# Layer 1's decay matrix: from summed terms and exponentials to spread factors and two scans

## The chip, the core and the metric

The kernel runs on one core of a Trainium2 chip, as one program. The metric is device time in microseconds (us); less is better. The engines are named as in the profile: PE (TensorE matmuls), PEld (its weight loads), DVE (VectorE), ACT (ScalarE), POOL (GpSimd), SP (SyncE, which here only issues DMA).

## The reference

The input is two images of 64 x 64 tokens with 256 channels. Two layers run one after the other, each adding its result to the normalized stream. The change is in layer 1 alone: two passes over the rows and the columns in turn (four calls of `_mamba2` in all), bidirectional, with 8 heads of 64 channels and a state of 64.

```python
def _ssd(xh, dt, A, Bm, Cm):
    cum = jnp.cumsum(dt * A, axis=1)
    diff = cum[:, :, None, :] - cum[:, None, :, :]
    decay = jnp.where(mask, jnp.exp(diff), 0.0)          # mask: lower triangle
    scores = jnp.einsum('bln,bsn->bls', Cm, Bm)[..., None] * decay * dt[:, None, :, :]
    return jnp.einsum('blsh,bshp->blhp', scores, xh)

def _mamba2(x, Win, Wconv, bconv, dt_bias, A_log, D, gn_w, Wout):
    zxbcdt = x @ Win
    z = zxbcdt[..., :DIN]
    xBC = silu(_causal_conv(zxbcdt[..., DIN:DIN + CONVDIM], Wconv, bconv))   # 4 taps
    ...
    dt = softplus(zxbcdt[..., -NHEADS:] + dt_bias)
    A = -jnp.exp(A_log)
    y = _ssd(xh, dt, A, Bm, Cm) + rev(_ssd(rev(xh), rev(dt), A, rev(Bm), rev(Cm)))
    y = y + D[None, None, :, None] * xh
    y = _rmsnorm(y.reshape(b, l, DIN) * silu(z), gn_w)
    return y @ Wout
```

For a sequence of 64 tokens and one head, the decay between two tokens is the product of the factors exp(dt * A) of the tokens between them, in both directions.

## The kernel before

All is fp32. Layer 0 comes first and is not touched by the change. Layer 1 works in 128 blocks: 4 calls (calls 0 and 2 read columns of the image, with a stride, calls 1 and 3 read rows) of 2 images of 16 blocks. A block is 4 sequences of 64 tokens, 256 tokens; two sequences make a pair (q = 0, 1), one on each half of the 128 partitions. In call 3 each block also loads a kept tensor (`y_load`), adds it in `residual` and stores the result.

A block is a list of steps. Each step issues a few instructions, all on one engine:

- PE: `norm_mean`, `x_proj` 0 and 1, `z_proj` 0 and 1, `bc_proj`, `dt_proj` (projections by `Win`), `scores`, `x_transpose` 0 and 1, `decay_sums` 0 and 1, `outputs` (64 small matmuls), `out_proj`, `out_mean`.
- ACT: `norm_squares`; `norm_factor` and `out_factor` (a Ln, then an Exp); `conv_start` and `bc_conv_start` (the last tap of the convolution); `dt_log` (Abs, Exp, Ln: three small instructions); `x_silu`, `z_silu`, `bc_silu` (Silu); `x_copy`; `decays` (Exp in place in PSUM); `out_squares`.
- DVE: `norm_scale`, `conv_taps` 0 and 1 and `bc_conv_taps` (the other three taps, 15 instructions in all, one line in the profile, L1114), `dt_bias`, `dt_sum` (one instruction for dt, then four small ones for `dta`, L1227), `scores_twice`, `mix`, `gated`, `out_scale`.
- POOL: `norm_total`, `decay_terms` (four multiplies of 128 x 512, L1259), `weights` 0 and 1 (a multiply, L1312, and an add, L1318, each), `out_total` (L1375, L1377), `residual` (L1417, in call 3 also L1419).

The decay matrix is made in three steps: `decay_terms` puts dt * A into a triangular mask (`within`), `decay_sums` sums it with matmuls against a second mask (`between`), and `decays` takes the exponential in PSUM. `mix` multiplies it by `weights`.

The order is written by hand in `STEPS`: each step has a time in hundredths of a block's period. Block i's step is issued at 100 i + that time, all blocks' steps sorted together, and every instruction is kept in that order on its engine (`pin`). So in the steady state the queue of an engine holds its steps sorted by time modulo 100, those with a larger time belonging to earlier blocks.

```python
todo = plan([Block(i) for i in range(8 * NBLK)], 100, STEPS)
todo += plan(weights, 2 * NBLK * 100, WEIGHTS, -8)
todo += plan([norm], 0, NORM, -4)
issue(todo)
```

`NORM` holds the group norm of the second image, which runs beside the first blocks: 16 statistics on DVE, 16 `apply` steps on ACT. `WEIGHTS` loads and scales the weights of a call. PSUM has 8 banks, which `bank()` hands out; a tile is given back after its last reader. ACT needs the table of a function loaded (ACT_TABLE_LOAD) before it; most loads are put in where the function that follows isn't in the table at hand, and a load of a common table for Ln and Exp is written out by hand at the end of `bc_silu` (L1251):

```python
pin(nc.scalar.preload_act_table_set(LOG_EXP))
```

Of the kernel before, what the change touches and what calls it, by code (L numbers as in the profile page):

```python
# [13 lines left out]
P = 128  # L14
C = 256
KT = C // P
L = 64
# [207 lines left out]
    (30, "norm_total"),  # L225
    (106, "norm_mean"),
    (129, "norm_factor"),
    (142, "norm_scale"),
    (148, "x_proj", 0),
    (149, "dt_proj"),  # L230
    (157, "conv_start", 0),
    (176, "x_proj", 1),
    (178, "conv_start", 1),
    (179, "dt_bias"),
    (188, "bc_proj"),
    (201, "conv_taps", 0),
    (201, "bc_conv_start"),
    (205, "dt_log"),
    (217, "z_proj", 1),
    (221, "z_proj", 0),  # L240
    (223, "conv_taps", 1),
    (230, "bc_conv_taps"),
    (243, "x_silu"),
    (246, "z_silu"),
    (248, "bc_silu"),
    (251, "x_transpose", 0),
    (252, "scores"),
    (256, "dt_sum"),
    (260, "x_transpose", 1),
    (265, "x_copy", 0),  # L250
    (271, "x_copy", 1),
    (274, "decay_terms"),
    (282, "scores_twice"),
    (287, "weights", 1),
    (289, "decay_sums", 1),
    (302, "decays", 1),
    (305, "decay_sums", 0),
    (313, "weights", 0),
    (315, "decays", 0),
    (324, "mix", 1),  # L260
    (329, "mix", 0),
    (332, "outputs"),
    (356, "gated"),
    (413, "out_squares"),
    (424, "out_total"),
    (428, "out_proj"),
    (448, "out_mean"),
    (454, "out_factor"),
    (460, "out_scale"),
    (480, "y_load"),  # L270
    (559, "residual"),
# [86 lines left out]
class Consts:  # L358
    def __init__(self, nc, pool):
        def tile_(shape, name):  # L360
            return pool.tile(shape, F32, name=name, tag=name)
# [40 lines left out]

        self.between = tile_([P, L], "between")
        self.within = tile_([P, L], "within")
        for t, op, mult in ((self.between, ALU.is_gt, 1), (self.within, ALU.is_ge, -1)):
            nc.gpsimd.memset(t, 1.0)
            for half, sign in ((0, mult), (1, -mult)):
                rows = t[half * L : (half + 1) * L, :]  # L410
                nc.gpsimd.affine_select(
                    out=rows,
                    in_=rows,
                    compare_op=op,
                    fill=0.0,
                    base=0,
                    pattern=[[-sign, L]],
                    channel_multiplier=sign,
                )
# [592 lines left out]
def layer1(tc, k, d, U, kept, out):  # L1012
# [7 lines left out]
    with ExitStack() as ctx:  # L1020
# [5 lines left out]
        ps = ctx.enter_context(tc.tile_pool(name="l1_ps", bufs=8, space=PSUM))  # L1026
        pin = tc.keep_in_program_order

# [6 lines left out]
        class Weights:  # L1035
# [5 lines left out]
            def load(self):  # L1041
# [14 lines left out]
                self.heads = wp.tile([P, 2, NH], F32, name="heads")  # L1056
                nc.sync.dma_start(out=self.heads, in_=d[self.ax + "_heads"][self.li : self.li + 1].to_broadcast([P, 2, NH]))
# [26 lines left out]
            def decay_rates(self):  # L1084
                self.neg_a = wp.tile([P, NH], F32, name="neg_a")
                act(self.neg_a, self.heads[:, 1, :], AF.Exp)
                pin(nc.vector.tensor_scalar(self.neg_a, self.neg_a, -1.0, None, ALU.mult))
# [22 lines left out]
        def taps(dst, pp, w):  # L1110
            dsts, pps = seqs(dst), seqs(pp)
            for j in range(1, TAPS):
                pin(
                    nc.vector.scalar_tensor_tensor(  # L1114
                        dsts[:, :, j:],
                        pps[:, :, : L - j],
                        w[:, TAPS - 1 - j : TAPS - j],
                        dsts[:, :, j:],
                        ALU.mult,
                        ALU.add,  # L1120
                    )
                )
# [4 lines left out]
        class Block:  # L1127
# [48 lines left out]
            def conv_taps(self, h):  # L1176
                for j in range(2):
                    c = 2 * h + j
                    taps(self.conv[:, c, :], half_of(self.px[h], j), self.w.cols[:, c, :])
# [8 lines left out]

            def bc_conv_taps(self):
                taps(self.conv_bc, self.pbc, self.w.bc_cols)  # L1190
# [16 lines left out]
            def dt_bias(self):  # L1207
                self.dt = two.tile([P, NPAIR, NH], F32, name="dt")
                bias = self.w.heads[:, 0:1, :].to_broadcast([P, NPAIR, NH])
                pin(nc.vector.tensor_add(self.dt, self.pdt, bias))  # L1210
# [7 lines left out]
            def dt_sum(self):  # L1218
                dt = self.dt
                pin(nc.vector.scalar_tensor_tensor(dt, dt, 0.0, self.log, ALU.max, ALU.add))  # L1220
                dta = two.tile([P, NPAIR, 2, NH], F32, name="dta")
                for e in range(2):
                    rows = slice(e * L, (e + 1) * L)
                    a = self.w.neg_a[rows].unsqueeze(1).to_broadcast([L, NPAIR, NH])
                    for half in range(2):
                        to = slice(half * L, (half + 1) * L)
                        pin(nc.vector.tensor_mul(dta[to, :, e, :], dt[rows], a))  # L1227
                self.dta = dta.rearrange("p q e h -> p (q e) h")
# [23 lines left out]


            def decay_terms(self):
                self.terms = []
                for s in range(SB):
                    terms = two.tile([P, NH, L], F32, name=f"terms{s}", tag=f"terms{s}")
                    pin(
                        nc.gpsimd.tensor_mul(  # L1259
                            terms,  # L1260
                            self.dta[:, s, :].unsqueeze(2).to_broadcast([P, NH, L]),
                            k.within.unsqueeze(1).to_broadcast([P, NH, L]),
                        )
                    )
                    self.terms.append(terms)
# [57 lines left out]
            def decay_sums(self, q):  # L1323
                self.seg = getattr(self, "seg", {})
                self.seg[q] = bank()
                for e in range(2):
                    matmul(
                        self.seg[q][e * L : (e + 1) * L],
                        k.between,
                        self.terms[2 * q + e].rearrange("p h l -> p (h l)"),  # L1330
                        True,
                        True,
                    )

            def decays(self, q):
                act(self.seg[q], self.seg[q], AF.Exp)

            def mix(self, q):
                self.mixes = getattr(self, "mixes", {})
                self.mixes[q] = two.tile([P, NH, L], F32, name=f"mix{q}", tag=f"mix{q}")  # L1340
                seg = self.seg[q].rearrange("p (h l) -> p h l", l=L)
                pin(nc.vector.tensor_mul(self.mixes[q], seg, self.weight[q]))
# [167 lines left out]
```

## Time and profile before

| | |
|---|---|
| median of 3 runs | 8551.74 us (8551.55 to 8555.54) |
| span of the profiled execution | 8553.2 us (no other time is given for it) |
| PE busy | 8258.4 us, 97% |
| DVE busy | 7426.7 us, 87% |
| ACT busy | 6797.4 us, 79% |
| POOL busy | 7588.4 us, 89% |
| chain that ended last, by line | PE L1033 25% of the span, PE L1273 2%, the rest under 1% each |

The profile is of one execution. Busy shares are means over both layers, so they are read by stage, in windows of the span. A group of instructions has a line of `kernel.py`, an engine, the operation and its tiles (output <- inputs); lines L1030 and L1033 are the helpers `act` and `matmul`, so there the tiles tell the step. fp32 matmuls have two records each, and their ends are modelled: on PE the time from one start to the next is read.

### The profile page before, as it was taken

The numbers are of one execution on the slowest core, as the hardware profiler recorded it, in microseconds if no ns is written. First come the engines' busy times: TensorE is split into PE (matmuls) and PEld (weight loads), VectorE is DVE, ScalarE is ACT, GpSimd is POOL, SyncE is SP. The second block draws the span as 40 slices with busy tenths as digits, with TensorE's granted clock in tenths as the row PEclk, the third lists the DMA queues.
The fourth block names the chain that finished last, engine by engine and source line by source line (L and its number), as shares of the span: only waits on it lengthen the run. The fifth ranks groups of instructions, "written<-read, shape, count | busy, mean of one in ns | idle before, by whom it ended". The sixth has DMA issues, their size and how long they took to land. (4 is left out here: it accounts for less than half of the span.)

```text
span 8553.2 us, 159162 instructions
## 1 busy us (share of the span) xinstructions
PE 8258.4 (97%) x60752; PEld 7001.5 (82%) x60752; DVE 7426.7 (87%) x7179; ACT 6797.4 (79%) x11826; POOL 7588.4 (89%) x4426
## 2 busy tenths in 40 slices
PE   8999999999999999999999999999889999999999
PEld 6888888888888888888888888888777777777777
DVE  6999999999999999999998999999977777777776
ACT  5888888888888778888887888888768777777776
POOL 6999999999999999999999999999957777777777
PEclk9999999999999999999999999999999999999999
DMA  4443444444444444444444444444410000000001
GB/s 137 137 137 128 135 137 136 137 132 134 138 129 133 149 140 155 130 134 136 136 131 132 139 134 136 130 132 136 145 53 1 7 4 1 10 1 1 16 31 33
DMA packets 495562, 878.17 MB, mean 103 GB/s; under 512 B 69200, under 2 KB 85584, under 8 KB 493264
## 3 DMA queue, kind: packets, MB, share of 16 engines
q1 hardware_dynamic: 479296, 846.29, 31.6%
q10 hardware_dynamic: 15504, 21.71, 0.8%
q8 instruction: 480, 7.86, 0.4%
q14 instruction: 282, 2.31, 0.1%
HBM read 844.71 MB, written 23.07 MB: 101 GB/s over the span
## 5 line engine op out<-in xcount | busy, mean ns | idle before, releaser
L876 POOL TENSOR_TENSOR prod<-prod,c_row 128x1024 f32<-128x1024 f32 x1280 | 3005.3, 2369 | 89.7 <-DVE prod L865 85.4
L846 POOL TENSOR_TENSOR b<-dtx,b_row 128x1024 f32<-128x1024 f32 x1024 | 2417.1, 2374 | 177.5 <-DVE prod L865 160.3
L538 PE MATMUL ps_y<-ident,prod 128*128 128x128 f32 x16384 | 2088.2, 276 | 65.8 <-POOL prod L876 53.2
L538 PEld LDWEIGHTS ps_y<-ident,prod 128*128 128x128 f32 x16384 | 1842.5, 142 | 295.3 <-POOL prod L876 139.8
L531 ACT ACTIVATE ps_h<-dt,neg_a 128x512 f32<-128x512 f32 x2048 | 1408.4, 688 | 471.0 <-DVE prod L879 360.2
L865 DVE TENSOR_TENSOR_SCAN prod<-ps_h,b 128x1024 f32<-128x1024 f32 x768 | 1732.0, 2275 | 55.7 <-POOL b L846 31.8
L531 ACT ACTIVATE b<-dt,neg_a 128x512 f32<-128x512 f32 x2048 | 1356.9, 711 | 79.7 <-DVE prod L865 77.0
L531 ACT ACTIVATE scaled<-dtxt,bt 128x256 f32<-128x256 f32 x2560 | 1089.5, 497 | 305.3 <-PE ps_h L538 294.2
L865 DVE TENSOR_TENSOR_SCAN ps_h<-b,ps_h 128x1024 f32<-128x1024 f32 x512 | 1170.3, 2286 | 143.1 <-PE ps_h L534 91.5
L865 DVE TENSOR_TENSOR_SCAN prod<-b,ps_h 128x1024 f32<-128x1024 f32 x512 | 1167.6, 2281 | 58.6 <-PE ps_h L538 35.2
L1033 PE MATMUL ps_mm<-xn,w_in 128*128 128x256 f32 x4608 | 1063.6, 381 | 12.9 <-DVE xn L1154 12.9
L879 DVE TENSOR_TENSOR prod<-ps_h,c_row 128x1024 f32<-128x1024 f32 x768 | 940.7, 1225 | 154.9 <-DVE ps_h L865 83.8
L1259 POOL TENSOR_TENSOR terms<-dta,within 128x512 f32<-128x512 f32 x512 | 524.0, 1044 | 541.8 <-DVE dta L1227 527.7
L1033 PEld LDWEIGHTS ps_mm<-xn,w_in 128*128 128x128 f32 x4608 | 868.9, 191 | 128.2 <-DVE xn L1154 13.9
L534 PE MATMUL ps_mm<-xi,diag_w 128*128 128x256 f32 (+3 forms) x4096 | 918.2, 374 | 1.5 <-ACT xi L531 1.5
L534 PE MATMUL ps_h<-diag,dtxt 128*128 128x128 f32 x6144 | 764.5, 278 | 90.1 <-DVE prod L879 61.3
L534 PEld LDWEIGHTS ps_h<-diag,dtxt 128*128 128x128 f32 x6144 | 724.7, 193 | 134.6 <-ACT ps_h L531 75.1
L534 PEld LDWEIGHTS ps_mm<-xi,diag_w 128*128 128x128 f32 x4096 | 753.1, 190 | 80.7 <-issue 1.5
L538 PE MATMUL ps_h<-ident,scaled 128*128 128x128 f32 x5120 | 693.3, 280 | 73.7 <-DVE prod L879 51.0
L1114 DVE SCALAR_TENSOR_TENSOR conv<-ps_mm,cols,conv 128x252 f32<-128x252 f32 (+2 forms) x1536 | 705.3, 474 | 63.9 <-ACT conv L1030 27.6
L538 PEld LDWEIGHTS ps_h<-ident,scaled 128*128 128x128 f32 x5120 | 583.0, 144 | 179.7 <-ACT b L531 71.1
L865 DVE TENSOR_TENSOR_SCAN ps_h<-ps_h,b 128x1024 f32<-128x1024 f32 x256 | 583.4, 2279 | 0.2 <-ACT ps_h L531 0.2
(144 smaller groups left out, 12212.5 us busy)
## 6 DMA issues: line engine op xcount, KB each, us to landing
c_row<-bc_rows SPq DMA_DIRECT2D x2048, 256.0 KB, 3.3
b_row<-bc_rows SPq DMA_DIRECT2D x1024, 256.0 KB, 3.3
y_in<-y SPq DMA_DIRECT2D x32, 256.0 KB, 2.9
out_dram<-y_in SPq DMA_DIRECT2D x32, 256.0 KB, 2.5
XU<-in_x_dram SPq DMA_DIRECT2D x8, 512.0 KB, 7.3
bc_rows<-dbc SPq DMA_DIRECT2D x128, 32.0 KB, 2.8
XU<-in_x_dram ACTq DMA_DIRECT2D x8, 512.0 KB, 5.5
y<-Y ACTq DMA_DIRECT2D x8, 512.0 KB, 5.1
```

What stands on the lines that cost most here:

```text
L531: pin(nc.scalar.activation(*args, **kwargs))
L534: pin(nc.tensor.matmul(out, lhsT=lhsT, rhs=rhs, start=start, stop=stop))
L538: nc.tensor.matmul(out, lhsT=x, rhs=order, start=start, stop=stop, is_transpose=True)
L846: pin(nc.gpsimd.tensor_mul(b, self.dtx[u], self.row(u, 0, n)))
L865: nc.vector.tensor_tensor_scan(*(t.rearrange("p c t -> p (c t)") for t in (to, a, b)), 0.0, ALU.mult, ALU.add,)
L876: pin(nc.gpsimd.tensor_mul(prod, prod, self.row(u, 1, n)))
L879: pin(nc.vector.tensor_mul(prod, self.h[u, n], self.row(u, 1, n)))
L1033: pin(nc.tensor.matmul(out, lhsT=lhsT, rhs=rhs, start=start, stop=stop))
L1114: nc.vector.scalar_tensor_tensor(dsts[:, :, j:], pps[:, :, : L - j], w[:, TAPS - 1 - j : TAPS - j], dsts[:, :, j:], ALU.mult, ALU.add,)
L1259: nc.gpsimd.tensor_mul(terms, self.dta[:, s, :].unsqueeze(2).to_broadcast([P, NH, L]), k.within.unsqueeze(1).to_broadcast([P, NH, L]),)
```

## The change

The matrix is now built from the factors. `dt_turn` transposes dt on PE, `factors` takes exp(dt * A) on ACT in one instruction of 16 partitions x 128, writes the rows to DRAM with two DMAs and reads them back with two more, each of which spreads a row of 16 x 65 numbers over 64 partitions (`spread`; the 65th number of each group is zero). `decay_after` runs along `spread` from a unit matrix (`units`) with a scan (multiply, then max), and `decay_before` runs a second one in the other direction over the result of the first. Both are DVE instructions of 128 x 1040. `mix` moves from DVE to POOL. `decay_terms`, `decay_sums`, `decays`, the four `dta` instructions and the masks `within` and `between` go. `taps` now goes through the tiles of a `conv_taps` step in turn, tap by tap, and the taps of `bc_conv_taps` are part of `conv_taps` 1. The loads of bias and rates in `Weights` are split in three. `STEPS` has new times throughout.

The diff, cut (removed masks, context and blank lines are left out):

```diff
@@ -222,53 +222,51 @@
 STEPS = (
     (0, "norm_squares"),
-    (30, "norm_total"),
-    (106, "norm_mean"),
-    (129, "norm_factor"),
-    (142, "norm_scale"),
-    (148, "x_proj", 0),
-    (149, "dt_proj"),
-    (157, "conv_start", 0),
-    (176, "x_proj", 1),
-    (178, "conv_start", 1),
-    (179, "dt_bias"),
-    (188, "bc_proj"),
-    (201, "conv_taps", 0),
-    (201, "bc_conv_start"),
-    (205, "dt_log"),
-    (217, "z_proj", 1),
-    (221, "z_proj", 0),
-    (223, "conv_taps", 1),
-    (230, "bc_conv_taps"),
-    (243, "x_silu"),
-    (246, "z_silu"),
-    (248, "bc_silu"),
-    (251, "x_transpose", 0),
-    (252, "scores"),
-    (256, "dt_sum"),
-    (260, "x_transpose", 1),
-    (265, "x_copy", 0),
-    (271, "x_copy", 1),
-    (274, "decay_terms"),
-    (282, "scores_twice"),
-    (287, "weights", 1),
-    (289, "decay_sums", 1),
-    (302, "decays", 1),
-    (305, "decay_sums", 0),
-    (313, "weights", 0),
-    (315, "decays", 0),
-    (324, "mix", 1),
-    (329, "mix", 0),
-    (332, "outputs"),
-    (356, "gated"),
-    (413, "out_squares"),
-    (424, "out_total"),
-    (428, "out_proj"),
-    (448, "out_mean"),
-    (454, "out_factor"),
-    (460, "out_scale"),
-    (480, "y_load"),
-    (559, "residual"),
+    (58.2, "norm_total"),
+    (58.6, "norm_mean"),
+    (100.9, "norm_factor"),
+    (108.4, "norm_scale"),
+    (112.4, "dt_proj"),
+    (118.4, "bc_proj"),
+    (132, "dt_bias"),
+    (141.2, "bc_conv_start"),
+    (145.8, "x_proj", 0),
+    (146.3, "dt_log"),
+    (149, "x_proj", 1),
+    (149.7, "z_proj", 1),
+    (151.9, "conv_start", 0),
+    (157.4, "conv_start", 1),
+    (167.2, "conv_taps", 0),
+    (172.6, "dt_sum"),
+    (189.8, "dt_turn"),
+    (199.9, "conv_taps", 1),
+    (217.3, "z_proj", 0),
+    (218.3, "factors"),
+    (224.8, "bc_silu"),
+    (271.8, "z_silu"),
+    (300.5, "scores"),
+    (316.3, "scores_twice"),
+    (319.8, "y_load"),
+    (320.1, "x_silu"),
+    (325, "weights", 1),
+    (327.2, "weights", 0),
+    (329.8, "decay_after"),
+    (336.1, "x_transpose", 0),
+    (341, "x_copy", 0),
+    (347.7, "x_transpose", 1),
+    (354.5, "x_copy", 1),
+    (362.7, "decay_before"),
+    (364.8, "mix", 0),
+    (393.3, "mix", 1),
+    (395.1, "outputs"),
+    (417, "gated"),
+    (427.2, "out_squares"),
+    (469.6, "out_proj"),
+    (514.4, "out_total"),
+    (529.4, "out_mean"),
+    (532.9, "out_factor"),
+    (534.3, "out_scale"),
+    (546.6, "residual"),
 )
...
@@ -1024,7 +1004,17 @@
+        dram = ctx.enter_context(tc.tile_pool(name="l1_dram", bufs=3, space=bass.MemoryType.DRAM))
+        units = one.tile([P, NPAIR * NH, L + 1], F32, name="units")
+        nc.vector.memset(units[:, :, L:], 0.0)
+        nc.vector.tensor_copy(
+            units[:, :, :L], k.eye.unsqueeze(1).to_broadcast([P, NPAIR * NH, L])
+        )
+        factors = [one.tile([NPAIR * NH, 2, L + 1], F32, name=f"factors{j}") for j in range(2)]
+        for t in factors:
+            nc.vector.memset(t, 0.0)
@@ -1053,8 +1043,14 @@
-                self.heads = wp.tile([P, 2, NH], F32, name="heads")
-                nc.sync.dma_start(out=self.heads, in_=d[self.ax + "_heads"][self.li : self.li + 1].to_broadcast([P, 2, NH]))
+                heads = d[self.ax + "_heads"][self.li]
+                self.bias = wp.tile([P, NH], F32, name="bias")
+                nc.sync.dma_start(out=self.bias, in_=heads[0:1].to_broadcast([P, NH]))
+                self.neg_a = wp.tile([NPAIR * NH, 1], F32, name="neg_a")
+                for q in range(NPAIR):
+                    nc.sync.dma_start(
+                        out=self.neg_a[q * NH : (q + 1) * NH], in_=heads[1:2].rearrange("o h -> h o")
+                    )
@@ -1082,8 +1078,7 @@
-                self.neg_a = wp.tile([P, NH], F32, name="neg_a")
-                act(self.neg_a, self.heads[:, 1, :], AF.Exp)
+                act(self.neg_a, self.neg_a, AF.Exp)
@@ -1107,19 +1102,20 @@
-        def taps(dst, pp, w):
-            dsts, pps = seqs(dst), seqs(pp)
+        def taps(parts):
-                pin(
-                    nc.vector.scalar_tensor_tensor(
-                        dsts[:, :, j:],
-                        pps[:, :, : L - j],
-                        w[:, TAPS - 1 - j : TAPS - j],
-                        dsts[:, :, j:],
-                        ALU.mult,
-                        ALU.add,
-                    )
-                )
+                for dst, pp, w in parts:
+                    to = seqs(dst)[:, :, j:]
+                    pin(
+                        nc.vector.scalar_tensor_tensor(
+                            to,
+                            seqs(pp)[:, :, : L - j],
+                            w[:, TAPS - 1 - j : TAPS - j],
+                            to,
+                            ALU.mult,
+                            ALU.add,
+                        )
+                    )
         def last_tap(dst, pp, w):
@@ -1174,9 +1170,10 @@
             def conv_taps(self, h):
-                for j in range(2):
-                    c = 2 * h + j
-                    taps(self.conv[:, c, :], half_of(self.px[h], j), self.w.cols[:, c, :])
+                parts = [(self.conv[:, 2 * h + j, :], half_of(self.px[h], j), self.w.cols[:, 2 * h + j, :]) for j in range(2)]
+                if h:
+                    parts.append((self.conv_bc, self.pbc, self.w.bc_cols))
+                taps(parts)
             def bc_proj(self):
@@ -1185,9 +1182,6 @@
             def bc_conv_start(self):
-            def bc_conv_taps(self):
-                taps(self.conv_bc, self.pbc, self.w.bc_cols)
@@ -1206,7 +1200,7 @@
             def dt_bias(self):
-                bias = self.w.heads[:, 0:1, :].to_broadcast([P, NPAIR, NH])
+                bias = self.w.bias.unsqueeze(1).to_broadcast([P, NPAIR, NH])
             def dt_log(self):
@@ -1218,14 +1212,44 @@
             def dt_sum(self):
-                dta = two.tile([P, NPAIR, 2, NH], F32, name="dta")
+            def dt_turn(self):
+                pa = self.pa = bank()[: NPAIR * NH, :P]
+                pin(nc.tensor.transpose(pa, self.dt.rearrange("p q h -> p (q h)"), k.ident))
+            def factors(self):
+                a = factors[self.i % 2]
+                act(
+                    a[:, :, :L],
+                    self.pa.rearrange("r (e l) -> r e l", l=L),
+                    AF.Exp,
+                    scale=self.w.neg_a,
+                )
+                rows = dram.tile([2, NPAIR, NH, L + 1], F32, name="factor_rows")
+                for q in range(NPAIR):
+                    nc.sync.dma_start(
+                        out=rows[:, q].rearrange("e h l -> h e l"), in_=a[q * NH : (q + 1) * NH]
+                    )
+                self.spread = two.tile([P, NPAIR * NH, L + 1], F32, name="spread")
-                    rows = slice(e * L, (e + 1) * L)
-                    a = self.w.neg_a[rows].unsqueeze(1).to_broadcast([L, NPAIR, NH])
-                    for half in range(2):
-                        to = slice(half * L, (half + 1) * L)
-                        pin(nc.vector.tensor_mul(dta[to, :, e, :], dt[rows], a))
-                self.dta = dta.rearrange("p q e h -> p (q e) h")
+                    row = rows[e : e + 1].rearrange("o q h l -> o (q h l)")
+                    nc.sync.dma_start(
+                        out=self.spread[e * L : (e + 1) * L].rearrange("p g l -> p (g l)"),
+                        in_=row.to_broadcast([L, NPAIR * NH * (L + 1)]),
+                    )
+            def decay_after(self):
+                self.decay = two.tile([P, NPAIR * NH, L + 1], F32, name="decay")
+                a, to, start = (
+                    t.rearrange("p g l -> p (g l)") for t in (self.spread, self.decay, units)
+                )
+                pin(nc.vector.tensor_tensor_scan(to, a, start, 0.0, ALU.mult, ALU.max))
+            def decay_before(self):
+                a, to = (
+                    t.rearrange("p g l -> p (g l)")[:, ::-1] for t in (self.spread, self.decay)
+                )
+                pin(nc.vector.tensor_tensor_scan(to, a, to, 0.0, ALU.mult, ALU.max))
             def z_proj(self, h):
@@ -1249,20 +1273,6 @@
-            def decay_terms(self):
-                self.terms = []
-                for s in range(SB):
-                    terms = two.tile([P, NH, L], F32, name=f"terms{s}", tag=f"terms{s}")
-                    pin(
-                        nc.gpsimd.tensor_mul(
-                            terms,
-                            self.dta[:, s, :].unsqueeze(2).to_broadcast([P, NH, L]),
-                            k.within.unsqueeze(1).to_broadcast([P, NH, L]),
-                        )
-                    )
-                    self.terms.append(terms)
             def x_transpose(self, q):
@@ -1320,26 +1330,11 @@
-            def decay_sums(self, q):
-                self.seg = getattr(self, "seg", {})
-                self.seg[q] = bank()
-                for e in range(2):
-                    matmul(
-                        self.seg[q][e * L : (e + 1) * L],
-                        k.between,
-                        self.terms[2 * q + e].rearrange("p h l -> p (h l)"),
-                        True,
-                        True,
-                    )
-            def decays(self, q):
-                act(self.seg[q], self.seg[q], AF.Exp)
             def mix(self, q):
-                seg = self.seg[q].rearrange("p (h l) -> p h l", l=L)
-                pin(nc.vector.tensor_mul(self.mixes[q], seg, self.weight[q]))
+                decay = self.decay[:, q * NH : (q + 1) * NH, :L]
+                pin(nc.gpsimd.tensor_mul(self.mixes[q], decay, self.weight[q]))
             def outputs(self):

```

## The prediction

> **What bounds the kernel now.** The time by stage comes first: layer 0 ends near 6250 us and the change is in layer 1, so I read busy time in windows there (us, then PE, PEld, DVE, ACT and POOL busy with their counts, the clock, the DMA share, GB/s).
>
> ```profile
> 7200.00:7600.00 400.00, 400.00 (x3408) 316.09 (x3407) 294.92 (x644) 314.94 (x568) 291.41 (x275) 1.00 0.02 6
> 7600.00:8000.00 400.00, 400.00 (x3467) 317.34 (x3466) 294.43 (x638) 317.30 (x564) 293.53 (x272) 1.00 0.01 1
> 8000.00:8400.00 400.00, 400.00 (x3393) 315.79 (x3392) 283.87 (x634) 310.03 (x569) 312.77 (x295) 1.00 0.09 29
> ```
>
> PE never stops, at full clock; DVE, ACT and POOL have a fifth to a quarter free. The chain of waits for 7500 to 7560 (start, length, what) is PE alone, and repeats itself.
>
> ```profile
> 7503.59 16.23 PE ps_mm L1033 x136
> 7519.82 0.49 PE ps_mm L1273 x4
> ...
> 7521.28 16.23 PE ps_mm L1033 x136
> 7537.51 0.49 PE ps_mm L1273 x4
> ```
>
> So a block costs 17.69 us (7537.51 - 7519.82), and 128 blocks 2264 us. Most of one block on PE, in the timeline (start, length, what; I count from start to start):
>
> ```profile
> 7506.11 1.94 PE L1033 MATMUL ps_mm<-terms,between 128*64 128x512 f32 x8
> 7507.98 0.70 PE L1033 MATMUL ps_mm<-total,mean_c 128*128 128x256 f32 x2
> 7508.52 3.62 PE L1033 MATMUL ps_mm<-xn,w_in 128*128 128x256 f32 x16
> 7511.97 3.62 PE L1033 MATMUL ps_mm<-yg,w_out 128*128 128x256 f32 x16
> 7515.52 1.16 PE L1033 MATMUL ps_mm<-mix,xt 64*64 64x64 f32 x64
> 7516.61 0.70 PE L1033 MATMUL ps_mm<-total,mean_di 128*128 128x256 f32 x2
> ```
>
> So decay_sums takes 1.87, norm_mean 0.54, one z_proj or x_proj 1.73 (half of the sixteen's 3.45), out_proj 3.55, outputs 1.09; from the rows left out, out_mean 0.53, dt_proj 0.81, bc_proj 0.90, each x_transpose 0.50, scores 0.45.
>
> Two more places of the timeline matter: Ln then Exp near the start, and dta beside POOL.
>
> ```profile
> 19.87 1.28 ACT L481 ACT_TABLE_LOAD   x1 [19.87 <-PE ps_mm L460]
> 21.16 0.26 ACT L481 ACTIVATE gn_log<-ps_mm,eps_gn 128x2 f32<-128x2 f32 x1
> 21.45 1.28 ACT L483 ACT_TABLE_LOAD   x1
> 22.74 0.20 ACT L483 ACTIVATE gn_scale<-gn_log 128x2 f32<-128x2 f32 x1
> ```
>
> ```profile
> 7518.70 0.94 DVE L1227 TENSOR_TENSOR dta<-dt,neg_a 64x16 f32<-64x16 f32 x1
> 7518.56 1.04 POOL L1259 TENSOR_TENSOR terms<-dta,within 128x512 f32<-128x512 f32 x1 [4.12 <-DVE dta L1227]
> ```
>
> Ln and the Exp behind it each load a table where no common one was put in place (L1251 does that); a load starts 0.03 after the instruction before it (21.16 + 0.26 to 21.45). And dta, both inputs in SBUF, median 0.17, takes 0.94: it ends 0.04 after the POOL instruction beside it. DVE instructions with an input in PSUM show no such stretch (scans 2.275 to 2.286 beside POOL's 2.37).
>
> **Part by part, us a block.**
>
> PE: minus 1.87; dt_turn adds one transpose, 0.12 to 0.2 by L1273's 0.49 for four: 0.15. Sum 15.97.
>
> ACT: minus two decays, 2 x 0.51 start to start; factors (16 partitions by 128) 0.2 to 0.4 by the log rows: 0.3. The order adds the large item. x_silu, z_silu and bc_silu stood together: one load, and one at L1251. Now, by time modulo 100, z_silu stands alone at 71.8; norm_factor (0.9), factors, x_silu (20.1) and bc_silu follow. That makes five loads: z_silu, Ln, Exp, x_silu, L1251. Three more at 1.29 are 3.87. ACT: 14.0 busy now (317.3/400 x 17.69) - 1.02 + 0.3 + 3.87 = 17.1.
>
> DVE: minus two mixes (0.69 each) and four dta (1.50). taps now interleaves tiles: two taps on one tile start 0.51 apart (7506.41, 7506.93, 7507.44), on different tiles 0.39 apart (7507.44, 7507.83); fifteen go from 7.05 to 5.85. Added: two scans of 1040 elements, 2.275 x 1040/1024 = 2.31 each. No row shows a scan with both inputs in SBUF; bounds are 1.24 (the plain multiply L879, scaled) and 3.59 (a POOL wait of 1.28 in front). I take 2.31, the same operation, and count waits apart. Sum about 13.6, no bound by itself.
>
> POOL: minus four terms (4.20), plus two mixes, 1.04 to 1.28 each (L1312, L1318); the latter reads two full tiles, as mix does.
>
> DMA: factors puts four transfers on SP's queue, the reads behind the landed writes: 2.8 (bc_rows) plus 3.3 (b_row, 3.0 to 7.2). At the slowest that is 2 x 7.2 = 14.4; decay_after comes 1.115 periods later, 19.7, so they cost nothing, and what they overran 19.7 by if that cover went. Queued behind them on SP are, in call 3, y_load (now before the store that frees its tile, so it waits for that) and the out store; the residual needs y two blocks later: nothing. Loads of bias and neg_a, four a call: nothing, WEIGHTS puts them fifteen blocks ahead. PSUM banks: 15 a block before (two decay_sums), 15 - 2 + 1 now without them and with dt_turn, but pz 1 is held for 1.2 periods and scores waits for one that conv_taps 1 frees; between nothing and scores' own 0.45, I take nothing, since PE reaches scores after conv_taps 1 ends.
>
> **The wait that replaces PE.** Both scans read SBUF twice, so by the dta row a scan and a POOL instruction exclude each other; all of POOL's work reads SBUF. (That POOL in turn waits for DVE no row shows plainly; nothing to the scan's 2.31 each, I take all of it, since dta waited for all of POOL's.) Then one stretch is serial. From the end of scores: score 0.29 + 0.05; weights 1 and 0, 2.36 each start to start: 4.72; both scans fall among them and the residual, 2.31 + 0.09 handover each: 4.80; residual 1.35 (call 3 adds 1.35 for y; calls 0 and 2, strided, 1.75); norm_total 0.78; then PE, which waits in norm_mean for it with all else queued behind: norm_mean 0.54, out_proj 3.55, dt_turn 0.15, outputs 1.09, scores 0.50. Sum 18.22 in calls 0 and 2; 17.82 in call 1; 19.17 in call 3.
>
> A second loop lies just below: z_silu 1.29 + 0.95, norm_squares 1.12 (calls 1, 3: 0.63), norm_factor 2 x 1.29 + 0.45 + 0.39, norm_scale 1.15 (0.78), PE from dt_proj to x_proj 1: 0.81 + 1.73 + 0.90 + 0.53 + 0.50 + 1.73 + 0.50 + 1.73 + 0.16 = 8.59, conv_start 1.02, handovers 0.15: 17.7 (16.8).
>
> Total: 64 x 18.22 + 32 x 17.82 + 32 x 19.17 = 2350, plus 86. Work that hid in slack: 16 applies at 0.80, 16 statistics at 0.70, weight scaling 5.4 a call, together 46; the cover is mostly gone, between 0 and 46, I take a third, 15. The profiled span 8553.2 then becomes 8654; it lies 1.5 above the median 8551.74 (only its span is given, no time around it), so 8652.
>
> [...]
>
> **The rivals.** (1) Faster: the scan does not shut POOL out. If more than 0.67 of the 4.80 (86/128) runs beside POOL, the loss is gone; with all of it, the second loop decides: 64 x 17.7 + 64 x 16.8 = 2208, so minus 56, plus 13 for the applies on a full ACT: 8509. For it: the shown block is a 16-element instruction, no scan. Against: its 0.94 ends with POOL's.
> (2) POOL, back to back, takes its next turn before the waiting scan. Then DVE is the loop: norm_scale 0.97, score 0.29, weights 4.72, scans 4.80, residual 1.75, taps 2.34, dt_sum 0.17 after about 1.0 behind a mix, taps 3.51: 19.55 (18.8 in call 1, 20.15 in call 3): 2498, so plus 233 and 15: 8800. The dta row doesn't say who is next, since that POOL instruction needed dta anyway.
> (3) The loads do not come (a common set is found for Ln and Exp) and POOL is not shut out: the second loop is 16.4 in calls 0 and 2, PE's 15.97 bounds 1 and 3: 64 x (16.4 + 15.97) = 2072, minus 192: 8360. L481 and L483 speak against it.
>
> **How the numbers follow.** Forecast 0.48, with its own range 8600 to 8720. Rival 1 0.19, rival 2 0.17, rival 3 0.06; 0.10 for losses and gains that meet within 0.2% (17 us, about what a measurement here can tell from no change). Faster: 0.19 + 0.06 = 0.25; slower: 0.48 + 0.17 = 0.65. The range, 8490 to 8800, takes in rival 1, the bounds on hidden work and the lower half of rival 2; outside are rival 3 (0.06), the other half of rival 2 (0.08) and a tail of rival 1 (0.03): 0.17.
>
> **What would show it.** Right: five table loads a block (640 in layer 1); PE busy falling to about nine tenths, with idle in front of norm_mean put down to POOL total; scans longer than 2.31 in the mean, or POOL weights longer than 1.28; call 3 the slowest and call 1 the fastest per block. Wrong: scans of 2.31 beside unstretched POOL instructions (rival 1); two or four loads a block; DVE without a pause while POOL idles (rival 2); or a wait on spread's transfers.

## The result, and the profile after

The changed kernel takes 8633.42 us (median of 4 runs, 8627.77 to 8640.51), against 8551.65 for the kernel before in the same series (4 runs): a ratio of 1.0093, 95% interval 1.0078 to 1.0107. It is slower by about 80 us. The forecast was 8652.

The same windows as before (us; PE, PEld, DVE, ACT, POOL busy with counts; clock, DMA share, GB/s), the profiled span being 8632.8:

```profile
7200.00:7600.00 400.00, 366.76 (x3321) 312.21 (x3319) 333.97 (x551) 385.30 (x618) 339.89 (x228) 0.98 0.13 37
7600.00:8000.00 400.00, 359.92 (x3307) 306.49 (x3308) 339.03 (x551) 388.80 (x612) 345.23 (x230) 1.00 0.12 32
8000.00:8400.00 400.00, 353.74 (x3065) 297.71 (x3064) 297.50 (x510) 356.24 (x577) 336.80 (x231) 0.95 0.18 53
```

PE was busy for all 400 us of each; now it stands for 33 to 46. ACT went from 317 to 389 and is the fullest engine in calls 1 and 2. In the third window, which lies in call 3, PE's clock is 0.95.

The chain of waits in call 2, the counterpart of PE's unbroken chain before (start, length, what; some short pieces are marked as left out):

```profile
7616.85 1.28 ACT L1020
7618.15 1.09 ACT gate L1020 x2
7619.23 1.00 ACT sq L1020
7620.25 1.28 ACT L1020
7621.55 0.45 ACT ps_mm L1020
7622.07 1.24 issue
7623.31 0.38 ACT ps_mm L1020
7623.71 1.04 DVE xn L1150
7624.78 4.18 PE ps_mm L1023 x22
...
7633.34 1.02 ACT conv L1020 x2
7634.38 1.28 ACT L1020
```

This is the prediction's second loop, piece by piece: a table load (an ACT row with no tile), `z_silu`, `norm_squares`, a load, Ln, a load ("issue"), Exp, `norm_scale`, PE from `dt_proj` to `x_proj` 1, `conv_start`. It closes in 17.53 us (7634.38 - 7616.85). In call 1 nearly all of the chain is ACT, from one load to the same load of the next block in 16.78. The table loads, on the page and, for L1275, in the groups of 6500 to 8300 (about 102 blocks):

```profile
L1020 ACT ACT_TABLE_LOAD x518 | 664.6, 1283 | 9.3
```

```profile
L1275 ACT ACT_TABLE_LOAD x102 | 130.9, 1283 | 1.8
L1328 POOL TENSOR_TENSOR weight<-weight,diag_d 128x512 f32<-128x512 f32 x203 | 462.8, 2280 | 15.9
L1252 DVE TENSOR_TENSOR_SCAN decay<-spread,decay 128x1040 f32<-128x1040 f32 x101 | 283.9, 2811 | 0.0
L1246 DVE TENSOR_TENSOR_SCAN decay<-spread,units 128x1040 f32<-128x1040 f32 x102 | 237.8, 2332 | 0.0
L1412 POOL TENSOR_TENSOR XU<-XU,res 128x512 f32<-128x512 f32 x53 | 183.2, 3456 | 1.2 <-DVE res L1397 1.2
```

Four loads a block on L1020 (518 is 4 x 128 and six others) and one on L1275: five, where there were two. POOL's add of `diag_d` takes 2.28 us in the mean (before 1.29), the residual 3.46 (1.43 before), and the second scan 2.81. The timeline of a block in call 2 shows why:

```profile
7608.53 2.30 DVE L1246 TENSOR_TENSOR_SCAN decay<-spread,units 128x1040 f32<-128x1040 f32 x1
7608.61 3.30 POOL L1328 TENSOR_TENSOR weight<-weight,diag_d 128x512 f32<-128x512 f32 x1
7611.87 1.04 POOL L1322 TENSOR_TENSOR weight<-score,dt 128x512 f32<-128x512 f32 x1
7612.99 1.28 POOL L1328 TENSOR_TENSOR weight<-weight,diag_d 128x512 f32<-128x512 f32 x1
7613.63 2.81 DVE L1252 TENSOR_TENSOR_SCAN decay<-spread,decay 128x1040 f32<-128x1040 f32 x1
7614.22 3.66 POOL L1412 TENSOR_TENSOR XU<-XU,res 128x512 f32<-128x512 f32 x1
7618.61 0.70 PE L1023 MATMUL ps_mm<-total,mean_c 128*128 128x256 f32 x2 [1.10 <-POOL total L1138]
```

The first scan runs undisturbed for 2.30, and the add that begins 0.08 after it ends 1.08 after the scan's end. The second scan begins while POOL's other add runs, ends 2.17 after it (so it waited first), and the residual that begins behind it stretches to 3.66. In these rows, where both want a turn, they alternate: neither goes twice while the other waits. PE then waits 1.10 for POOL's `norm_total`.

Per block (from one `norm_scale` to the next, means over 16 blocks, 15 in the last, call by call):

| | call 0 | call 1 | call 2 | call 3 | last `norm_scale` to end |
|---|---|---|---|---|---|
| before | 17.55, 17.66 | 17.69, 17.72 | 17.69, 17.66 | 17.69, 17.69 | 50.5 |
| after | 19.45, 17.54 | 17.33, 16.91 | 18.04, 17.55 | 18.80, 19.03 | 72.0 |

So the gain is there, small, in the later blocks of calls 0 to 2; it is lost in the first 16 blocks (+30 us), in call 3 (+38), and after the last block (+21.5). Calls 0 to 2 behind the first 16 blocks give 17 back. The first `norm_scale` came 6.6 later, at 6265.4 against 6258.8; that is no cost of the change, since layer 0 is the same and its end moves by itself from run to run (in e7_warm, which differs from the changed kernel in call 3 alone, the first `norm_scale` comes at 6250.7). 30.4 + 38 + 21.5 + 6.6 - 17 = 79.5, of the 79.6 between the spans.

Call 3 has a loss that the prediction did not know of. Behind its first five its blocks take either 18.1 or 19.8 us, a little over half of them 19.8. Timeline of two, then windows of 2 us:

```profile
8328.97 0.70 PE L1023 MATMUL ps_mm<-total,mean_c 128*128 128x256 f32 x2 [2.31 <-POOL total L1138]
8329.50 5.30 PE L1023 MATMUL ps_mm<-yg,w_out 128*128 128x256 f32 x16
8348.75 0.70 PE L1023 MATMUL ps_mm<-total,mean_c 128*128 128x256 f32 x2 [2.31 <-POOL total L1138]
8349.28 3.62 PE L1023 MATMUL ps_mm<-yg,w_out 128*128 128x256 f32 x16
```

```profile
8330.00:8332.00 2.00, 2.00 (x7) 1.62 (x6) 1.72 (x5) 1.97 (x3) 2.00 (x3) 0.60 0.19 58
8332.00:8334.00 2.00, 2.00 (x7) 1.58 (x6) 0.69 (x1) 1.01 (x2) 1.15 (x2) 0.55 0.46 131
8350.00:8352.00 2.00, 2.00 (x11) 1.77 (x10) 1.49 (x4) 1.97 (x3) 2.00 (x2) 1.00 0.06 18
```

Both blocks stand 2.31 us for `norm_total`. In one, `out_proj` takes 5.30 behind it, at a granted clock of 0.60 and 0.55; in the next it takes its 3.62 at 1.00.

### The profile page after: what moved, and what is told of

Same layout as the page of the kernel before. It is cut to its first block, busy times and chain, and to the rows that moved or that the text cites. A ratio compares the mean times of both kernels' runs of the same rounds, so it can differ in the third digit from the quotient of the medians.

```text
span 8632.8 us, 158117 instructions
## 1 busy us (share of the span) xinstructions
PE 8081.3 (94%) x59856; PEld 6981.1 (81%) x59856; DVE 7649.2 (89%) x6671; ACT 7198.5 (83%) x12090; POOL 7868.5 (91%) x4164
## 5 line engine op out<-in xcount | busy, mean ns | idle before, releaser
L1023 PE MATMUL ps_mm<-xn,w_in 128*128 128x256 f32 x4608 | 1101.5, 390 | 0.0
L1110 DVE SCALAR_TENSOR_TENSOR conv<-ps_mm,cols,conv 128x252 f32<-128x252 f32 (+2 forms) x1536 | 627.0, 460 | 14.8 <-ACT conv L1020 14.8
L1328 POOL TENSOR_TENSOR weight<-weight,diag_d 128x512 f32<-128x512 f32 x256 | 580.4, 2267 | 20.1
```

The lines of the kernel that those rows point to most:

```text
L1023: pin(nc.tensor.matmul(out, lhsT=lhsT, rhs=rhs, start=start, stop=stop))
L1110: nc.vector.scalar_tensor_tensor(to, seqs(pp)[:, :, : L - j], w[:, TAPS - 1 - j : TAPS - j], to, ALU.mult, ALU.add,)
L1328: pin(nc.gpsimd.tensor_add(w, w, self.w.diag_d))
```

## The experiments

Theory 1 rests on the prediction: scans and POOL shut each other out, which makes a serial stretch from `scores` to `norm_mean`, and the lone `z_silu` with its table loads makes a second loop of about the same length. Times per block by call and half call are read as in the table above. The rivals: the shutting out counts for nothing, the loads alone count, or the new order alone does.

**Tables: e1_silus_together.** `z_silu` stands behind `bc_silu`, and the load of the common table behind both: two loads a block instead of five.

```diff
     (224.8, "bc_silu"),
-    (271.8, "z_silu"),
+    (224.9, "z_silu"),
@@ bc_silu
-                pin(nc.scalar.preload_act_table_set(LOG_EXP))
@@ z_silu, at its end
+                pin(nc.scalar.preload_act_table_set(LOG_EXP))
```

> The changed kernel with z_silu issued right behind bc_silu and the common table loaded after it, so two table loads a block in place of five. Theory 1 (two bounds: ACT with five loads in calls 0 to 2 and in the first 16 blocks, the serial stretch of scans and POOL in call 3): ACT falls from about 17 to 13.2 us a block; calls 0 to 2 then stand at the stretch, about 17.1 and 16.7, the first 16 blocks fall from 19.45 to about 17.7, call 3 stays near 19.0. In all about 8580. Theory 2 (the loads are the whole loss, in call 3 too): every block falls to PE's 16.0, about 8360. Theory 3 (the scans on DVE are the loss): no change, 8633.

Measured: 8611.48 us, 1.0069 of before (1.0049 to 1.0089), 22 less than the changed kernel where 53 were expected. The later blocks of calls 0 to 2 stay at 17.4 and 17.0; the first 16 fall from 19.45 to 17.92, 24 us, and that is the gain. Call 3 loses some 12 us of it (19.24 and 19.38 in its halves, at a clock of 0.94 from 8000 to 8400). The chain of waits in call 2 has changed:

```profile
7616.95 0.30 DVE score L1313
...
7617.32 1.05 POOL weight L1322
...
7618.44 3.29 POOL weight L1328
7621.73 1.01 POOL weight L1322
...
7622.81 1.27 POOL weight L1328
...
7624.37 2.21 POOL XU L1412
...
7627.90 0.76 POOL total L1138
...
7628.70 4.15 PE ps_mm L1023 x18
```

With the second loop gone, this is the prediction's first: score, the two weights with a scan inside the first add, the residual behind the second scan, `norm_total`, PE. It closes in 17.37 (the next score begins at 7634.32). So in calls 0 and 2 the two loops were within 0.2 us of each other, and taking one away could not help by more. In call 1 the first loop is not seen alone: the chain there, 16.9 long, goes from `z_silu` through ACT's rows to `norm_total` and PE.

**Turns on POOL: e2_total_early.** `norm_total` before the weights instead of behind the residual.

```diff
-    (58.2, "norm_total"),
+    (14.5, "norm_total"),
```

> The changed kernel with norm_total at 14.5 in place of 58.2, so that it runs on POOL ahead of weights and residual, and norm_mean on PE waits for neither scans nor residual. Theory 1: only call 3 was bound by that stretch; it falls from 19.0 to about 17.0, PE's idle before norm_mean goes and its clock stays at 1.0; calls 0 to 2 keep 17.5 and 16.8 (ACT). About 8565. Theory 2 (table loads alone): nothing, 8633. Theory 3 (DVE): nothing, 8633.

Measured: 8629.56 us, 1.0091 (1.0073 to 1.011): no gain, where 8565 was expected. The total is that of theories 2 and 3, but not for their reason. Call 3 fell as expected, from 18.8 and 19.0 (its two halves) to 17.6 and 17.1. Calls 0 and 2 rose instead, to 18.6 and 18.7 in their later halves, with blocks of 17.5, 19.2 and 20.9 mixed: the second loop still holds PE, its stop now falls in one piece in front of `dt_proj` (waits for xn of up to 2.0 us), and the mean clock in the window 7600 to 8000 is 0.93 instead of 1.00. The 19.2 and 20.9 are 1.7 and 3.4 above 17.5, which would be one and two stretches of low clock at the price of call 3's (5.30 - 3.62). So what call 3 won, calls 0 to 2 lost.

**Both loops: e3_both.** The two edits together.

> Both edits at once: z_silu behind bc_silu with two table loads, and norm_total early. Theory 1: with both bounds gone PE's own 15.97 is next, 16.0 to 16.5 a block, about 8375 in all, faster than both kernels. Theory 2: the same as with the silus together alone. Theory 3 (DVE, 13.6 of work and its waits for POOL): above 17 a block, over 8500.

Measured: 8514.01 us, 0.9958 (0.9944 to 0.9971), faster than before, but not the expected 8375; the total lies in theory 3's range (DVE, over 8500). Later blocks: 17.2, 17.3, 17.1 and 16.2. That both must go for a gain is what two loops of one length predict. What was left, in the waits of 6900 to 7200, in call 1 (total, times, longest):

```profile
PEld ps_mm L1023 <- DVE xn L1150: 27.7, 17, 1.7
PE ps_mm L1023 <- DVE xn L1150: 25.3, 17, 1.5
```

PE stops once a block in front of `dt_proj`; DVE works on the taps of `conv_taps` 1 while `norm_scale` is ready to go (in one block of call 2 the Exp of `norm_factor` ends at 7721.31 and `norm_scale` begins at 7724.60). In calls 0 and 2 every fourth or fifth block then takes 18.3 instead of 16.7, again at a lower clock (0.63 and 0.52 in the windows 7726 to 7730, behind a stop of 1.12).

**DVE's order: e5_scale_first.** e3_both with `conv_taps` 1 behind `norm_scale`.

```diff
-    (199.9, "conv_taps", 1),
+    (208.5, "conv_taps", 1),
```

> e3_both with conv_taps 1 (its nine taps, 3.5 us of DVE) put behind norm_scale instead of in front of it. In e3_both the last stop of PE is 1.1 us in front of dt_proj for xn, because DVE still works on these taps when norm_factor is done; after such stops some blocks take 18.3 us instead of 16.7. Theory (PE's stop is only DVE's order): the stop goes, the period falls to PE's own work, 16.0 to 16.2 in all calls, and the total from 8514 to about 8430 us. Rival (x_silu, bc_silu and z_silu only move later by the same 1 us, and PE then stops in front of x_transpose or z_silu's bank): no change, 8500 to 8530 us.

Measured: 8454.44 us, 0.9883 (0.9865 to 0.9901), 1.2% faster than before and 2.1% faster than the change as made; 24 above the expected 8430, outside the rival's range. The period is 16.3 in calls 0 and 2 and 16.2 in call 3 (PE's own sum was put at 15.97); call 1 keeps 16.7 and 17.5 in turn. So what was left was DVE's order and not the length of its work. The theory holds but for call 1, where PE waits for a bank that `conv_taps` 1 now frees later (11.6 us in 18 waits on DVE conv, 6900 to 7200).

**The second SBUF input: e9_psum_scans.** e1_silus_together with the scans' second input read from PSUM. The decay matrix is then not the reference's.

```diff
+        def scan_halves(blk, to, a, second):
+            last = blk.n == 8 * NBLK - 1
+            for h in range(2):
+                cols = slice(512 * h, 512 * h + 512)
+                b = second[:, cols] if last else blocks[blk.n + 1].pz[1]
+                pin(nc.vector.tensor_tensor_scan(to[:, cols], a[:, cols], b, 0.0, ALU.mult, ALU.max))
@@ decay_after
-                pin(nc.vector.tensor_tensor_scan(to, a, start, 0.0, ALU.mult, ALU.max))
+                scan_halves(self, to, a, start)
@@ decay_before
-                pin(nc.vector.tensor_tensor_scan(to, a, to, 0.0, ALU.mult, ALU.max))
+                scan_halves(self, to, a, a)
```

(`pz[1]` is the PSUM bank of the next block's `z_proj` 1; 1024 of the 1040 elements are scanned. The numbering of the blocks is left out.)

> e1_silus_together with the second input of both scans read from PSUM (a live bank of the next block's z_proj 1) instead of SBUF, each scan as two of 512 elements. The decay values are not the reference's; all other work stays. Theory 1 (a scan with two SBUF inputs and a POOL instruction shut each other out): POOL's add of diag_d falls from a mean of 2.28 to 1.28 us, the residual to between 1.4 and 1.8, each half scan takes 1.14 to 1.2, the period falls from 17.4 (call 3: 19.3) to 16.1 to 16.6 everywhere and the total from 8611 to about 8440 us. Rival (the scans' 4.6 us of DVE time themselves set the stretch, not the port): times of the POOL instructions and the period as in e1_silus_together, 8595 to 8625 us.

Measured: 8461.07 us, 0.9891 (0.9876 to 0.9906), 150 less than e1_silus_together. Its groups of 6500 to 8300:

```profile
L1128 DVE TENSOR_TENSOR_SCAN decay<-spread,ps_mm 128x512 f32<-128x512 f32 x430 | 500.2, 1205 | 84.8 <-ACT gate L1020 84.8
L1336 POOL TENSOR_TENSOR weight<-weight,diag_d 128x512 f32<-128x512 f32 x215 | 274.3, 1276 | 16.9
L1420 POOL TENSOR_TENSOR XU<-XU,res 128x512 f32<-128x512 f32 x55 | 78.9, 1434 | 142.9 <-DVE res L1405 142.9
```

A little more scan time per block (4 x 1.205 = 4.82 against 2.31 + 2.39), with the add back at 1.28 and the residual at 1.43. The period is 16.5 in calls 0 and 2 with some of 18.1, 16.2 in call 1 and 16.3 in call 3. So here it is the second SBUF input that costs, more than the scans' length. Part of the 150 is the clock that PE's stops had lowered: in e1_silus_together it is 0.94 from 8000 to 8400 and a matmul of `out_proj` takes 395 ns in the mean of 6500 to 8300, here 379, as in the kernel before. The residual now waits for `out_scale` on DVE instead, 2.6 us each time (142.9 in the 55 of its row). This is the one direct test of what the prediction took from the dta row, and both directions of it are now in rows: POOL's add 3.30 beside a scan of 2.30, and a scan of 2.81 behind a POOL add.

**The clock: e7_warm.** Four matmuls of constants in front of `norm_mean`, in call 3 alone.

```diff
                 self.pm = bank()[:, :TB]
+                if self.call == 3:
+                    for _ in range(4):
+                        matmul(self.pm, k.mean_c, units[:, :4, :L], True, True)
                 matmul(self.pm, k.mean_c, self.total, True, True)
```

> The changed kernel with four more matmuls of constants in front of norm_mean in call 3 alone (1.7 us of PE; their result is overwritten by norm_mean). There PE stands 2.3 us in front of norm_mean, and in every second block the rows after it run at a granted clock of 0.5 to 0.67. Theory (the stop lowers the clock, and the lower clock makes blocks of 19.8 us beside those of 18.1): with the stop cut to 0.6 us the clock stays at 1.0, all blocks of call 3 take 18.1, and the total falls by 16 x 1.7 = 27 us to about 8605. Rival (POOL's two adds of call 3 set the 19.8, the clock is no cause): still 18.1 and 19.8 in turn, 8633 us, or with the matmuls on the path 8633 + 32 x 1.7 = 8690.

Measured: 8601.87 us, 1.0056 (1.0037 to 1.0075), 32 less than the change as made, by adding 1.7 us of PE work to each of 32 blocks. In the two profiles 24 us of the difference lie in call 3's blocks (18.28 and 18.02 in its halves, against 18.80 and 19.03), and 15 ahead of the first `norm_scale`, where the kernels are the same. The timeline of call 3:

```profile
8322.11 1.89 PE L1023 MATMUL ps_mm<-units,mean_c 128*128 128x256 f32 x8
8324.59 0.70 PE L1023 MATMUL ps_mm<-total,mean_c 128*128 128x256 f32 x2 [0.58 <-POOL total L1138]
8325.12 3.62 PE L1023 MATMUL ps_mm<-yg,w_out 128*128 128x256 f32 x16
```

The stop is down to 0.58, `out_proj` takes 3.62 behind it (at 8307.03 as at 8325.12), the mean clock from 8000 to 8400 is 1.00, and behind the first five the blocks take 18.1. The lower clock was the cause of the 19.8.

**The order: e4_old_order.** The new decay matrix in the order of before. The edit is shown against the list of before; `conv_taps` 1 stands at 230 with the taps of `bc_conv_taps` in it.

```diff
     (256, "dt_sum"),
+    (257, "dt_turn"),
+    (259, "factors"),
     ...
-    (274, "decay_terms"),
-    (289, "decay_sums", 1),
-    (302, "decays", 1),
-    (305, "decay_sums", 0),
-    (315, "decays", 0),
+    (300, "decay_after"),
+    (312, "decay_before"),
```

> The new way to make the decay matrix, with the step order of before: dt_turn 257, factors 259, decay_after 300, decay_before 312 put in, decay_terms, decay_sums, decays taken out, taps of bc in conv_taps 1 at 230. The silus stand together there (two loads) and norm_total (30) is far ahead of norm_mean (106). Theory 1 (the loss is made by the order, which splits the silus and puts norm_total behind the residual): 16.0 to 16.6 a block, about 8380. Rival (the scans against POOL cost more than PE wins, in any order): 8633 or more.

Measured: 9370.38 us, 1.0962 (1.0936 to 1.0988), 23.9 us a block. Theory 1's own figure for this run, about 8380, was far off. The total lies in the rival's range, but its reason does not hold: e3_both and e5_scale_first have the same scans and are faster than before. Waits, 7700 to 8000:

```profile
DVE decay L1246 <- DMA spread<-factor_rows: 78.3, 12, 8.6
```

Twelve blocks, 6.5 us each: with 0.41 of a period between `factors` and `decay_after` the transfers are not hidden.

**The same, a period later: e8_old_order_late and e11_late_gates.** e4_old_order with `scores` to `residual` 100 later; `gated` at 445.5 and two buffers for the gate in e8_old_order_late, at 456 and three in e11_late_gates. Both hold three buffers of `dt` instead of two, and e11_late_gates one of each mix instead of two.

```diff
-    (252, "scores"),
+    (352, "scores"),
     ...
-    (300, "decay_after"),
+    (400, "decay_after"),
     ...
-    (559, "residual"),
+    (659, "residual"),
```

> e4_old_order (the new decay matrix in the order of before: 23.9 us a block) with everything from scores to residual one whole period later, so that two scans come 1.41 periods behind factors instead of 0.41; the order of the steps modulo 100 stays, but gated stands 0.1 of a period earlier. Theory (in the old order the transfers' 6 to 7 us and the chain dt_sum, factors, transfers, scans, mix, outputs inside one period are what costs): DVE no longer waits for spread, and the period falls to 17.5 to 19, the total from 9370 to 8560 to 8750. Rival (the old order itself, with scans in front of the weights, is at fault): above 21 us a block, over 9000.

Measured: 9012.18 us, 1.0532 (1.0508 to 1.0556), about 21.1 a block. The waits on spread are gone, and 2.8 us a block with them; the rest stays, in the rival's range. But the edit had brought a wait of its own, `z_silu` on a gate buffer (up to 5.8 us), so this run alone doesn't settle it.

> e8_old_order_late with a third buffer for gate, gated back at its old place behind z_silu, and one buffer instead of two for each mix, to make room. In e8_old_order_late z_silu waited up to 5.8 us for gated, since only two gates are held. Theory A (that wait, new in e8, is what keeps the block at 21 us): the period falls to 17.5 to 18.5, the total from 9012 to 8580 to 8700 us. Theory B (the old order puts outputs of one block right in front of the next block's scores on PE; score 0.34, weights 4.72, two scans 4.8 in turn with POOL, out_total 2.0, mix 2.35, outputs 1.1, then out_mean, z_proj 0, dt_proj, x_transpose and scores 4.8 make one serial chain of about 20): the period stays at 20 to 21 and the total above 8880 us.

Measured: 8896.39 us, 1.0414 (1.0392 to 1.0435), 20.2 to 20.5 a block. That is theory B's range. The timeline of its chain:

```profile
7765.55 2.99 POOL L1322 TENSOR_TENSOR weight<-score,dt 128x512 f32<-128x512 f32 x1 [5.04 <-DVE score L1313]
7769.85 3.20 POOL L1322 TENSOR_TENSOR weight<-score,dt 128x512 f32<-128x512 f32 x1
7776.40 2.31 POOL L1337 TENSOR_TENSOR mix<-decay,weight 128x512 f32<-128x512 f32 x2
7778.76 1.16 PE L1023 MATMUL ps_mm<-mix,xt 64*64 64x64 f32 x64 [3.05 <-POOL mix L1337]
```

`mix` of a block comes 10.9 us behind its first weight, with both scans' stretches and `out_total` in between on POOL, which is busy without a pause from 7765.55 to 7778.71; `outputs` waits 3.05 for it, and the next `scores` stands behind `outputs`, `out_mean`, `z_proj` 0 and `dt_proj` on PE. In the new `STEPS` both mixes run beside `out_proj` and `out_total` comes later still, so neither is on the chain (compare the 17.37 of e1_silus_together). The new order is thus needed twice: to hide the transfers, which e4_old_order and e8_old_order_late show, and to shorten the chain that the scans make, which is read from these rows and was not tested by an edit of its own.

**Taps: e10_taps.** The kernel before with the taps taken in turn and `bc_conv_taps` inside `conv_taps` 1.

```diff
-    (223, "conv_taps", 1),
-    (230, "bc_conv_taps"),
+    (230, "conv_taps", 1),
@@ taps: the loop over the tiles inside the loop over the taps
```

> The kernel before with one part of the change alone: the taps of the two tiles of conv_taps 1 and of conv_bc in turn instead of tile by tile, bc_conv_taps inside conv_taps 1. Theory (two taps on one tile start 0.51 apart, on two tiles 0.39; DVE is no bound there, PE is): DVE busy falls by about 1.2 us a block, the period stays 17.69 and the total within 0.2% of before. Rival (DVE's order counts, since conv_taps frees banks for PE): faster by 10 to 30 us.

Measured: 8550.87 us, ratio 1.0000 (0.9990 to 1.0011). DVE busy fell from 294.43 to 275.47 us in the window 7600 to 8000, 0.84 us a block (expected 1.2), and the period stayed 17.69.

## Why the prediction was right, and where its sum was not

The sign and the mechanisms hold. The total is 8633 against 8652, but that small difference is in part luck, since larger ones cancel: the 128 blocks were put about 50 us too slow (+101 with the hidden work; the table's means give 2314 against 2262, +53), and 28 us lie where no term was (21.5 after the last block, and 6.6 ahead of the first, in which the change has no part).

- **Serial stretch, 18.22 in calls 0 and 2: mis-sized.** e1_silus_together shows it alone, at 17.37. The weights and the first scan take 6.76 (7.12 in the sum), the second scan and the residual 3.82 (4.15), PE's part 5.62 (5.83). Each scan was charged with its 2.31 and a handover of 0.09; it costs POOL about 2.0 (3.30 - 1.28): the failed term is the handover, which is an overlap of 0.3 instead. The 17.82 of call 1 has no measurement.
- **Second loop, 17.7 and 16.8: hit.** 17.53 in call 2, 16.78 in call 1. As the first loop was over-sized, this one decides in calls 0 to 2, not the one named; the order of the two was the step that failed.
- **Call 3, 19.17: right by accident.** The stretch with the second residual is 18.09 (e7_warm); the rest of the measured 18.8 to 19.0 is the lower clock, which no term had.
- **Five table loads: hit.** Ln and the Exp behind it loaded a table each (1.28), as rows L481 and L483 said. Rival 3's 16.4 for the second loop, which is 17.7 less one load of 1.29, was an estimate that no run shows: with a load for each of the two the loop closed in 17.53.
- **Rival 2, POOL first each time: excluded** by the alternating turns of the timeline. Rival 1 is what e9_psum_scans makes by hand, without the extra loads: there the second SBUF input is worth 150 us, with the clock that its stops cost.
- **Transfers at nothing: hit**, for the distance given: from 6500 to 8300 no engine waits for `spread`. The prediction's condition, that they cost what they overrun once the cover is gone, is what e4_old_order shows.
- **Hidden work, 15 us: under-sized.** The first 16 blocks alone lost 30. With two loads instead of five they lose 6, so most of it goes with the loads, on an ACT that also had 16 `apply` steps to do. The clock has a part in it that no run separates: from 6262 to 6540 it is 0.88, against 0.98 before and 0.93 with two loads.
- **Last blocks: no term.** From the last `norm_scale` to the end takes 72.0 us instead of 50.5. The step list is longer there (4.38 periods to `residual` instead of 4.17), and the last blocks have no other work to hide loads and scans; the clock is 0.81 from 8546 on (0.93 from 8480 to 8553 before). No experiment separated these, and e5_scale_first keeps 72.

## What to carry to other kernels

When one bound is taken away, price every loop just below it: here two were 0.2 us apart, either edit alone gave 22 and 4 us, and both with one DVE step moved gave 2.1%. The scans with two SBUF inputs took POOL's time as well as DVE's own (an add of 1.28 became 3.30); reading one input from PSUM gave 150 us in e9_psum_scans, and where that is possible it is worth trying before reordering. And a stop on PE cost more than its length where the clock fell behind it (2.31 us, and 1.68 more in `out_proj`), so it can pay to fill it: e7_warm gained 32 us.

## What the runs showed of the hardware that was not expected

- **PE's clock falls after short stops, at times that shift against the blocks.** Behind a stop of 2.31 us `out_proj` takes 1.68 longer (5.30 - 3.62) in a little over half of call 3's blocks. Windows of half a us give a granted clock of 0.89 from 8330 to 8330.5, 0.50 in each from there to 8333.5, and 0.70 in the next: half rate for 3.4 us. Stretches at half rate in call 3 begin at 8309.91, 8330.39, 8367.94, 8405.48 and 8443.03, which is 6 or 11 times 3.413 us apart (20.48 and 37.55; 3.413 is 20.48 / 6), though the blocks are 18.1 and 19.8 long: they come 0.43 to 1.42 behind the start of `norm_mean`. With stops of 0.58 the mean clock from 8000 to 8400 is 1.00 (e7_warm). The length of a stop alone does not decide: e3_both lost the clock behind stops of 1.12, in every fourth or fifth block of call 2 (0.96 from 7400 to 7700), and kept 1.00 from 6900 to 7200 in call 1 with stops of 1.5; in call 2 of the changed kernel PE stands 1.10 in each block at 1.00. Where in the 3.4 us a stop falls may be what decides; that is not shown.
- **Scans and POOL take turns**, and the waiting one is recorded as busy: POOL's add of 1.28 shows as 3.30 beside a scan of 2.30, and the scan behind POOL's other add as 2.81. A stretched mean in the groups (the add 2.28, before 1.29; the second scan 2.81, 2.31 in the sum) is the sign of it here, where the waits show nothing.
